# Turning heads and maxima ahead of the projection inside a unit's side work, in an attention and feed-forward block on one core

## The chip, the core and the metric

The kernel runs on one core of a Trainium2 chip. The metric is the device time of one execution in microseconds (us), lower is better. Runs of the kernel before gave 5343.15, 5345.61 and 5349.25 us; their median is 5345.61 us.

The core has five engines with instruction streams of their own. The short names are those of the profile: PE does the matrix products and PEld is its weight load, DVE works on vectors, ACT applies functions, POOL is the general engine and SP only issues transfers here. A matrix product lands in one of the eight banks of the accumulator memory, each 128 partitions by 512 float32, and DVE or ACT reads it from there.

## The reference

The block is pre-normalised attention and then a feed-forward part. The attention has two softmaxes over half heads whose difference is applied to the values:

```python
qkv = x @ w_qkv                                  # x: 8 x 1024 x 512, layer-normed; 16 heads of 32
q1, q2 = split(q); k1, k2 = split(k)             # 16 wide each
a1 = softmax(q1 k1^T * scale); a2 = softmax(q2 k2^T * scale)
lam = exp(lq1 . lk1) - exp(lq2 . lk2) + 0.8
out = (a1 - lam * a2) @ v
out_n = out / sqrt(mean(out^2) + 1e-6) * norm_w * 0.2
x = x + out_cat(out_n) @ wo
```

The feed-forward part rounds its weights to three values, adds a low-rank term, squares a relu and multiplies by a second rounded matrix. The change does not touch it.

## The kernel before

Attention is cut into 256 units: a unit is one batch row, one head and one half (512) of its queries. A unit goes over its 1024 keys in 8 chunks of 128, and the main loop (L561) takes two chunks a step, so a unit has four steps, kc = 0, 2, 4, 6. The order of all instructions on PE, ACT, DVE and POOL is the order in which the loop writes them; nothing is reordered by a scheduler.

Every step has the same main work. `exp_scores` (L253) makes two score tiles for each chunk, one for each softmax: a product that spreads the row maxima (`nms`) over the tile and a product of keys and queries on top of it, both in L267; ACT takes the exponentials (L273). `max_scores` (L197) runs two units ahead: products of the same kind in L207 whose row maxima DVE takes in L218. POOL adds the exponentials up (L283, L285). `values` (L296, product in L290 into `acc`) multiplies the exponentials of the step before by the values.

The first step of a unit, kc = 0, also carries side work, collected in the list `posts`. A side job issues its PE instructions when it is called, and returns a closure with its ACT, DVE and transfer instructions, which all run in the same order at the end of the step:

- `project` (L151, 4 products of 512 columns, which the profile counts as 8 matmuls in L157), then ACT scales (L164), DVE makes the remainder (L165) and SP writes it out. It belongs to the next batch row. `value_tile` (L142, L145) is the same size on PE, with one ACT copy (L149) behind it. Both are marked `long`.
- `max_turn` (L230): one transpose (L232) of the maxima of the next unit, two DVE instructions (L236, L237), one transfer out and two back into `nms`.
- `heads_out` (L318): four transposes (L324) of the output and sums of the unit three before, then two reciprocals, two products and an addition on DVE (L334, L337, L347).
- `sums` (L310): products with ones (L290 into `one`), then an ACT copy (L316).
- `turn_tile` (L134): four transposes (L137) and an ACT copy. It is not `long` and comes last.

`prepare` (L399) lists 35 side steps for a batch row: 3 without PE work, then 8 pairs of a turned tile and a value tile, then 16 projections. One is taken at each kc = 0, and one more at kc = 4 of the 17th, 21st, 25th and 29th unit of a row (L589). The first of these four is a turned tile, the other three are projections, and the side work of kc = 4 has neither maxima nor heads. So a row has 8 value tiles and 13 projections at kc = 0; seven rows are prepared this way, which makes 56 and 91 such steps. Seven turned tiles a row, 49 in all, also lie at kc = 0, and in 27 further steps of kc = 0 with maxima, heads and sums there is no side step of `prepare`. In the last batch row half of the units (`light`, L275) carry two heads or none.

All score tiles and all side jobs draw their banks from one pool of four (`one_bank`, L104). The two chunks of a step take four tiles, so all four banks; the next tile asked for takes the bank of the first score tile, the next that of the second, and so on. A PE instruction that starts a tile therefore waits until the tile that had the bank before has been read. The products of `max_scores` have a pool of three banks of their own, the accumulator `acc` has one.

Of the kernel before, what the change touches and what calls it, by code (L numbers as in the profile page):

```python
# [24 lines left out]
def block_phases(  # L25
# [22 lines left out]
    NU = B * H * 2  # L48
# [55 lines left out]
    def one_bank():  # L104
        return ps_1.tile([P, 512], F32, tag="one", name="one")
# [71 lines left out]
    def load_keys(g):  # L177
        b, h = divmod(g, H)
        tk_of[g] = p_tk.tile([P, S], F32R, tag="tk", name="tk")
        src = qk_of[b][1, h * HD : (h + 1) * HD]  # L180
        for i in range(2):
            nc.sync.dma_start(
                tk_of[g][i::2].bitcast(F32), src[:, i : i + 1, :].to_broadcast([HD, 2, S])
            )

    def load_queries(u):
        b, h = divmod(u // 2, H)
        cols = slice((u % 2) * HS, (u % 2) * HS + HS)
        tq_of[u] = p_tq.tile([P, HS], F32R, tag="tq", name="tq")
        src = qk_of[b][0, h * HD : (h + 1) * HD, :, cols].rearrange("r i t -> (r i) t")  # L190
        for i in range(2):
            nc.sync.dma_start(tq_of[u][i::2].bitcast(F32), src)
# [4 lines left out]
    def max_scores(u, i, apart=False):  # L197

        c, kh = divmod(i, 2)
        if i == 0:  # L200
            nm_of[u] = p_s.tile([P, 2, 2, 4], F32, tag="nm", name="nm", bufs=2)
        mx = [ps_mx.tile([P, 512], F32, tag="mx", name="mx") for _ in range(2)]
        tq, tk = tq_of[u], tk_of[u // 2]

        def product(sm):
            rows = slice(64 * sm, 64 * sm + 64)
            nc.tensor.matmul(  # L207
                mx[sm], tq[rows, c * P : (c + 1) * P],
                tk[rows, kh * 512 : kh * 512 + 512], start=True, stop=True,
            )  # L210

        product(0)
        if not apart:
            product(1)

        def post():
            for sm in range(2):
                nc.vector.tensor_reduce(  # L218
                    nm_of[u][:, kh, sm, c : c + 1], mx[sm], AX.X, ALU.max, negate=True
                )  # L220
            if i == 7:
                nm = nm_of.pop(u)
                nm2_of[u] = p_s.tile([P, 8], F32, tag="nm2", name="nm2", bufs=2)
                nc.vector.tensor_reduce(
                    nm2_of[u], nm.rearrange("p k s c -> p (s c) k"), AX.X, ALU.min
                )

        return (lambda: product(1), post) if apart else post

    def max_turn(u):  # L230
        tr = one_bank()
        nc.tensor.transpose(tr[0:8, 0:P], nm2_of.pop(u), ident)  # L232

        def post():
            mt = p_s.tile([8, 2, P], F32R, tag="mt", name="mt", bufs=2)
            nc.vector.tensor_copy(mt[:, 0, :], tr[0:8, 0:P])  # L236
            nc.vector.tensor_sub(mt[:, 1, :], tr[0:8, 0:P], mt[:, 0, :].bitcast(F32))  # L237
            md = dpool.tile([2, 4, 2, P], F32, tag="md", name="md", bufs=4)
            nc.sync.dma_start(md.rearrange("s c a t -> (s c) a t"), mt.bitcast(F32))
            for sm in range(2):  # L240
                nc.sync.dma_start(
                    nms[u % 3][64 * sm : 64 * sm + 2].bitcast(F32)
                    .rearrange("a (c t) -> a c t", c=4),
                    md[sm].rearrange("c a t -> a c t"),
                )

        return post
# [31 lines left out]
    def add_up(u, kc):  # L279
        e = e_of[u, kc // 2]  # L280
        if kc == 2:
            es_of[u] = p_es.tile([P, 2, 2, HS], F32, tag="es", name="es")
            nc.gpsimd.tensor_add(es_of[u], e_of[u, 0], e)  # L283
        elif kc == 4 or kc == 6 and not light(u):
            nc.gpsimd.tensor_add(es_of[u], es_of[u], e)  # L285
# [19 lines left out]
    def evict(u):  # L305
        avs_of[u] = p_s.tile([P, 2, HS // 2], F32, tag="avs", name="avs", bufs=4)

        nc.scalar.activation(avs_of[u][:, 0, :], acc_of.pop(u), AF.Copy, scale=one_nlam)
# [47 lines left out]
    def rms_squares(n):  # L356
        sq_of[n] = p_y.tile([P, 4, P], F32, tag="sq", name="sq")
        nc.scalar.activation(sq_of[n], og_of[n], AF.Square)

    def rms_sums(n):  # L360
        ss_of[n] = p_s.tile([P, 16], F32, tag="ss", name="ss")
        nc.vector.tensor_reduce(
            ss_of[n], sq_of.pop(n).rearrange("p c (g d) -> p (c g) d", d=HD), AX.X, ALU.add
        )
# [10 lines left out]
    def output_rows(n, bank=one_bank):  # L375
        b, hp = divmod(n, NHP)
        xr = p_y.tile([P, E], F32, tag="xr", name="xr")
        rows = x[b].rearrange("(d r) e -> r d e", d=HD)
        for r in range(4):
            nc.sync.dma_start(xr[32 * r : 32 * r + 32, :], rows[4 * hp + r])  # L380
        py = bank()
        for c in range(KC):
            nc.tensor.matmul(  # L383
                py, og_of[n][:, c, :], wo_sb[:, c, :],
                start=(c == 0), stop=(c == KC - 1),
            )

        def post():
            y = p_y.tile([P, E], F32, tag="y", name="y")
            nc.vector.scalar_tensor_tensor(y, py, nw[:, hp : hp + 1], xr, ALU.mult, ALU.add)  # L390
            nc.sync.dma_start(x1_dram[n // 4][n % 4], y)

        return post
# [46 lines left out]
    with tc.tile_pool(name="a_stage", bufs=1) as stage, tc.manual_schedule(engines=engines):  # L440
# [26 lines left out]
        for i, step in enumerate(steps):  # L467
# [4 lines left out]
            posts = [step()]  # L472
# [7 lines left out]
            if i >= heads:  # L480
                um, im = divmod(i - heads, NS)
# [78 lines left out]
    with tc.tile_pool(name="a_e", bufs=5) as p_e, tc.tile_pool(name="a_es", bufs=2) as p_es:  # L560
        for s in range(0, NS * NU + 2, 2):  # L561
            u, kc = divmod(s, NS)
            um, im = divmod(s + AHEAD, NS)
            if done is not None:
                evict(done)
                done = None
            if u > NU - 2 * H and kc == 0:
                prep.fetch()
            if um < NU:
                if im == 0 and um + 1 < NU:  # L570
                    if um % 2 == 1:
                        load_keys(um // 2 + 1)
                    load_queries(um + 1)
                between, first = max_scores(um, im, apart=True)
            else:
                between = first = None
            if u < NU:
                if u % (2 * H) == 0 and kc == 0:
                    assert not fill
                    fill = prepare(u // (2 * H) + 1) if u + 2 * H < NU else prepare_tokens()  # L580
                exp_scores(u, kc, between=between)
                if first:
                    first()
                exp_scores(u, kc + 1)
                add_up(u, kc)
            reduce = max_scores(um, im + 1) if um < NU else None
            posts = []

            if fill and (kc == 0 or kc == 4 and u % (2 * H) >= H and u % 4 == 0):  # L589
                prepare_step, long = fill.pop(0)  # L590
            else:
                prepare_step = None
            if prepare_step and long:
                posts.append(prepare_step())
            if kc == 0 and um <= NU:
                posts.append(max_turn(um - 1))
            for v in outs.pop((u, kc), []):
                posts.append(heads_out(v))
                if v % 4 == 3:
                    n = v // 4  # L600
                    later[u, 6] = lambda n=n: rms_squares(n)
                    later[u + 1, 0] = lambda n=n: rms_sums(n)
                    later[u + 1, 2] = lambda n=n: rms_apply(n)
                    later[u + 2, 4] = lambda n=n: output_rows(n)
            if (u, kc) in later:
                posts.append(later.pop((u, kc))())
            for v in adds.pop((u, kc), []):
                posts.append(sums(v))
            if prepare_step and not long:
                posts.append(prepare_step())  # L610
            if reduce:
                reduce()
            if 2 <= s < NS * NU + 2:
                uv, kv = divmod(s - 2, NS)
                values(uv, kv)
                values(uv, kv + 1)
                if kv == NS - 2:
                    done = uv
            for post in posts:
                if post:  # L620
                    post()
        evict(done)
        prep.fetch_rest()
        whole(lambda: sums(NU - 1))
# [441 lines left out]
```

## Time and profile before

| What | Value |
|---|---|
| median of three runs | 5345.61 us |
| profiled execution, its own time | 5346.45 us |
| span in the profile | 5344.5 us |
| granted PE clock over the span | 0.999 |
| PE busy | 5277.1 us, 99% |
| DVE busy | 3786.5 us, 71% |
| ACT busy | 2834.1 us, 53% |
| POOL busy | 4128.1 us, 77% |
| of the span, attention steps of the main loop | about 145 to 4260 us |

The span is the time from the first to the last instruction of the program; the profiled execution took 1.95 us more than that. A line of a timeline gives the start in us from the start of the span, the length, the engine (SPq for a transfer issued by SP), the source line, the operation, what it writes and reads, its size and how many equal instructions are merged in the line; in brackets stands the idle time of the engine before it and what ended that time. A line of the waits gives who waited for whom, the total in us, how many times, and the longest.

### The profile page before, as it was taken

How to read it: one execution, taken by the hardware profiler on the slowest of the kernel's cores; microseconds unless marked ns; L12 is line 12 of the kernel's file. 1: busy time of each engine (PE TensorE's matmuls, PEld its weight loads, DVE VectorE, ACT ScalarE, POOL GpSimd, SP SyncE). 2: the span in 40 equal slices, each digit the busy share in tenths (PEclk: the TensorE clock that was granted, in tenths of full speed). 3: DMA queues.
4: the chain of work that ended last, by engine and by line, in shares of the span. 5: the costliest groups of instructions: out<-in, count | busy, mean ns of one | idle time of the engine just before them, and what ended most of it. 6: DMA issues, size and time to landing. Idle time of an engine off the chain costs nothing.

```text
span 5344.5 us, 105614 instructions
## 1 busy us (share of the span) xinstructions
PE 5277.1 (99%) x41522; PEld 3244.8 (61%) x41522; DVE 3786.5 (71%) x7599; ACT 2834.1 (53%) x5502; POOL 4128.1 (77%) x1511
## 2 busy tenths in 40 slices
PE   8999999999999999999999999999999999999999
PEld 4555555555555555555555555555555588788887
DVE  6877787777778777877777777777888545555554
ACT  4665566566656665666566656655666522222221
POOL 0998899889988998899899989998888733333333
PEclk9999999999999999999999999999999999999999
DMA  8112211221121112111211121112211101111111
GB/s 275 49 52 77 69 51 54 75 71 50 55 79 63 52 55 77 64 55 59 77 59 53 63 74 61 52 65 77 97 48 47 60 18 32 32 32 32 32 32 32
DMA packets 185247, 328.49 MB, mean 61 GB/s; under 512 B 33312, under 2 KB 55840, under 8 KB 184112
## 3 DMA queue, kind: packets, MB, share of 16 engines
q1 hardware_dynamic: 183824, 319.12, 18.7%
q8 instruction: 329, 5.39, 0.4%
q0 software_dynamic: 544, 2.10, 0.1%
q14 instruction: 166, 1.36, 0.1%
q10 hardware_dynamic: 384, 0.52, 0.0%
HBM read 209.16 MB, written 112.46 MB: 60 GB/s over the span
## 4 chain that ended last, share of the span: by engine, by line
PE 80%; POOL 12%; DVE 2%; issue 2%; ACT 1%; DMA 1%; SPq 0%; POOLq 0%; DVEq 0%; ACTq 0%
PE acc L290 15%; PE one L267 13%; PE mx L207 12%; PE one L157 8%; PE y L722 7%; POOL es L285 7%; PE pf L708 7%; PE one L290 4%; PE one L145 4%; PE one L383 3%; POOL es L283 3%; PE one L324 2%; DVE nm L218 1%; PE pf L709 1%; ACT e L273 1%
## 5 line engine op out<-in xcount | busy, mean ns | idle before, releaser
L218 DVE TENSOR_REDUCE nm<-mx 128x1 f32<-128x512 f32 x4096 | 2548.4, 682 | 257.6 <-PE mx L207 252.1
L273 ACT ACTIVATE e<-one 128x512 f32<-128x512 f32 x4096 | 2116.8, 602 | 802.8 <-PE one L267 750.5
L285 POOL TENSOR_TENSOR es<-es,e 128x2048 f32<-128x2048 f32 x495 | 2262.6, 4571 | 62.0 <-ACT e L273 30.0
L207 PE MATMUL mx<-tk,tq 64*128 64x512 f32 x4096 | 1451.2, 444 | 6.7 <-DVE nm L218 5.5
L283 POOL TENSOR_TENSOR es<-e 128x2048 f32<-128x2048 f32 x256 | 1170.0, 4570 | 277.1 <-ACT e L273 277.1
L267 PE MATMUL one<-nms,one 64*128 64x512 f32 x4096 | 1177.4, 420 | 4.6 <-ACT e L273 2.7
L290 PE MATMUL acc<-e,v 128*32 128x256 f32 x16384 | 1092.6, 384 | 0.0
L207 PEld LDWEIGHTS mx<-tk,tq 64*128 64x128 f32 x4096 | 751.0, 184 | 546.9 <-DVE nm L218 311.5
L267 PE MATMUL one<-tq,tk 64*128 64x512 f32 x4096 | 1065.0, 393 | 0.0
L712 POOL TENSOR_TENSOR r<-r 128x512 f32<-128x512 f32 x256 | 269.0, 1052 | 644.4 <-ACT r L711 636.7
L290 PEld LDWEIGHTS acc<-e,v 128*32 128x32 f32 x16384 | 450.1, 109 | 433.7 <-issue 177.3
L267 PEld LDWEIGHTS one<-tq,tk 64*128 64x128 f32 x4096 | 580.4, 185 | 83.2
L711 ACT ACTIVATE r<-pf,s_fc 128x512 f32<-128x512 f32 x256 | 176.5, 689 | 793.1 <-PE pf L709 555.8
L267 PEld LDWEIGHTS one<-nms,one 64*128 64x128 f32 x4096 | 515.8, 184 | 79.9 <-DVE og L347 14.7
L722 PE MATMUL y<-wpr,r 128*128 128x512 f32 x2048 | 523.7, 397 | 3.3 <-DVE r L716 1.5
L715 DVE CAST r<-r 128x512 fp32r<-128x512 f32 x256 | 179.0, 699 | 421.9 <-POOL r L712 421.8
L157 PE MATMUL one<-hT,wqk 128*128 128x512 f32 x1024 | 472.8, 605 | 0.0
L722 PEld LDWEIGHTS y<-wpr,r 128*128 128x128 f32 x2048 | 374.8, 188 | 98.6 <-DVE o L732 20.1
L708 PE MATMUL pf<-hTh,wfc 128*128 128x512 f32 x1024 | 399.3, 390 | 0.0
L708 PE MATMUL pf<-hTl,wfc 128*128 128x512 f32 x1024 | 398.9, 390 | 0.0
L165 DVE SCALAR_TENSOR_TENSOR pc<-one,pc 128x512 fp32r<-128x512 f32 x128 | 88.5, 691 | 344.4 <-ACT pc L164 344.4
L157 PEld LDWEIGHTS one<-hT,wqk 128*128 128x128 f32 x1024 | 184.1, 189 | 213.9 <-issue 186.4
(133 smaller groups left out, 4291.6 us busy)
## 6 DMA issues: line engine op xcount, KB each, us to landing
qk<-pc SPq DMA_DIRECT2D x128, 512.0 KB
tk<-qk SPq DMA_DIRECT2D x256, 256.0 KB
tq<-qk SPq DMA_DIRECT2D x512, 128.0 KB
xs<-in_L_attn_x SPq DMA_DIRECT2D x64, 256.0 KB
xr<-in_L_attn_x SPq DMA_DIRECT2D x256, 64.0 KB
x_dram<-y SPq DMA_DIRECT2D x64, 256.0 KB
out<-o SPq DMA_DIRECT2D x248, 64.0 KB
nms<-md SPq DMA_DIRECT2D x512, 4.0 KB
```

The lines of the kernel that those rows point to most:

```text
L145: nc.tensor.matmul(pv, hT_of[b][:, kc, c * P : (c + 1) * P], wv[:, kc, :], start=(kc == 0), stop=(kc == KC - 1),)
L157: nc.tensor.matmul(ps, wqk[:, kc, c0 : c0 + P], hT_of[b][:, kc, tok], start=(kc == 0), stop=(kc == KC - 1),)
L207: nc.tensor.matmul(mx[sm], tq[rows, c * P : (c + 1) * P], tk[rows, kh * 512 : kh * 512 + 512], start=True, stop=True,)
L218: nc.vector.tensor_reduce(nm_of[u][:, kh, sm, c : c + 1], mx[sm], AX.X, ALU.max, negate=True)
L267: nc.tensor.matmul(st[sm], w[rows, cols], m[rows, :], start=(w is one2), stop=(w is not one2))
L273: nc.scalar.activation(e[:, kc % 2, sm, :], st[sm], AF.Exp)
L283: nc.gpsimd.tensor_add(es_of[u], e_of[u, 0], e)
L285: nc.gpsimd.tensor_add(es_of[u], es_of[u], e)
L290: nc.tensor.matmul(out[32 * g : 32 * g + 32, :], w, e[:, g // 2, (g % 2) * (HS // 2) : (g % 2 + 1) * (HS // 2)], start=start, stop=stop,)
L708: nc.tensor.matmul(pf, w[:, kc, :], hT, start=(kc == 0 and i == 0), stop=False)
L712: nc.gpsimd.tensor_mul(r, r, r)
L722: nc.tensor.matmul(ys[i], r2[:, i * P : (i + 1) * P], prep.wpr[j // (NJ // 2)][:, j % (NJ // 2), :], start=(j == 0 and k == 0), stop=(j == ...
```

## The change

Within the side work of a step, `heads_out` is now called first, `max_turn` second, and the long step of `prepare` (a projection or a value tile) third, just ahead of `later` and `sums`. Before, the long step came first, then `max_turn`, then `heads_out`. The order of the closures moves in the same way, so also that of the DVE, ACT and SP instructions behind them. No instruction is added or removed.

```diff
             else:
                 prepare_step = None
-            if prepare_step and long:
-                posts.append(prepare_step())
-            if kc == 0 and um <= NU:
-                posts.append(max_turn(um - 1))
             for v in outs.pop((u, kc), []):
                 posts.append(heads_out(v))
                 if v % 4 == 3:
...
                     later[u + 2, 4] = lambda n=n: output_rows(n)
+            if kc == 0 and um <= NU:
+                posts.append(max_turn(um - 1))
+            if prepare_step and long:
+                posts.append(prepare_step())
             if (u, kc) in later:
                 posts.append(later.pop((u, kc))())
             for v in adds.pop((u, kc), []):
```

## The prediction

> **What bounds the kernel now.** I read the page first, then the waits of PE and DVE, then timelines of single steps.
>
> ```profile
> PE 5277.1 (99%) x41522; PEld 3244.8 (61%) x41522; DVE 3786.5 (71%) x7599; ACT 2834.1 (53%) x5502; POOL 4128.1 (77%) x1511
> ...
> PEclk9999999999999999999999999999999999999999
> ...
> DVE mt L236 <- PE one L232: 154.0, 57, 4.1
> DVE pc L165 <- ACT pc L164: 344.4, 121, 3.9
> PE one L145 <- ACT e L273: 10.7, 12, 1.5
> ```
>
> PE is never idle for long and its clock is full. The long waits are DVE's: it stands behind the projection (344 us, and 154 us before the maxima), with 71% work, so its waits matter only where PE then waits for DVE. A busy PE can still hide held-up instructions, because ends of matmuls are modelled. So I read starts. This is one first step of a unit with a projection, on PE, up to the step after the next:
>
> ```profile
> 1014.93 0.50 PE L207 MATMUL mx<-tk,tq 64*128 64x512 f32 x1
> ...
> 1016.64 3.70 PE L157 MATMUL one<-hT,wqk 128*128 128x512 f32 x8
> 1020.18 0.27 PE L232 MATMUL one<-ident,nm 128*8 128x128 f32 x1
> 1020.29 0.60 PE L324 MATMUL one<-ident,avs 128*128 128x128 f32 x4
> 1020.82 1.07 PE L290 MATMUL one<-es,ones 128*32 128x256 f32 x16
> 1021.70 1.05 PE L290 MATMUL acc<-e,v 128*32 128x256 f32 x16
> 1022.68 0.49 PE L207 MATMUL mx<-tk,tq 64*128 64x512 f32 x1
> ...
> 1025.49 0.50 PE L207 MATMUL mx<-tk,tq 64*128 64x512 f32 x1
> ```
>
> The step takes 7.75 us and every piece follows the last at once: 1.71 main products, 3.54 projection, 0.11 maxima, 0.53 heads, 0.88 sums, 0.98 values. The step behind it takes 2.81 us here, 2.74 in most units (1006.78 to 1009.52), against 2.70 for a plain step (1009.52 to 1012.22). The excess is DVE coming late from the side work. So PE sets the time, and a change of order can matter only through what PE must wait for.
>
> ACT in the same step, its four exponentials and then the third alone, and a step without a projection, where PE visibly waits:
>
> ```profile
> 1015.76 2.06 ACT L273 ACTIVATE e<-one 128x512 f32<-128x512 f32 x4
> 1016.74 0.60 ACT L273 ACTIVATE e<-one 128x512 f32<-128x512 f32 x1
> ...
> 665.04 1.08 ACT L273 ACTIVATE e<-one 128x512 f32<-128x512 f32 x2
> 665.41 0.27 PE L232 MATMUL one<-ident,nm 128*8 128x128 f32 x1
> 665.68 0.42 PEld L324 LDWEIGHTS one<-ident,avs 128*128 128x128 f32 x4 [0.19 <-ACT e L273]
> 665.68 0.66 PE L324 MATMUL one<-ident,avs 128*128 128x128 f32 x4
> 666.27 1.07 PE L290 MATMUL one<-es,ones 128*32 128x256 f32 x16
> ```
>
> Side tiles take the four score banks in turn, so the first needs the first exponential read, the second the second, and so on. In the lower step the maxima are first and the heads second. The second exponential starts at 665.04 and takes 0.60, so it ends at 665.64 (0.01 less if it is 0.59 long); the load of the heads starts at 665.68, 0.05 later, and not 0.11 after the maxima as in the upper step. That is the wait to watch. In the upper step the projection, first in line and 3.54 us long, covers exponentials two to four.
>
> **The change part by part.** Nothing is added or removed on any engine; all is order.
>
> *The 147 steps with a long job (91 projections, 56 value tiles).* Measured from the step's first L207, in us. The heads now start where the projection did, at 1.71: the first exponential has ended at 1015.76 + 0.60 - 1014.93 = 1.43. Their four transposes start 0.11 apart ((0.60 - 0.27) / 3), and the first, whose load nothing covers, costs 0.06 more (0.66 against 0.60 in the two rows). So the maxima follow after 4 x 0.11 + 0.06 = 0.50, at 2.21 (the second exponential is over at about 1.91), and the long job could start at 2.32. But it is third, and the third exponential ends at 1016.74 + 0.60 - 1014.93 = 2.41. With 0.05 for the signal it starts at 2.46: 0.14 of standing.
>
> How long it is then, up to the sums, comes from a step where a projection is followed by an output product of the same size:
>
> ```profile
> 1043.10 3.70 PE L157 MATMUL one<-hT,wqk 128*128 128x512 f32 x8
> 1046.64 3.60 PE L383 MATMUL one<-wo_sb,og 128*128 128x512 f32 x8
> 1050.16 1.07 PE L290 MATMUL acc<-e,v 128*32 128x256 f32 x16
> ```
>
> The first takes 3.54, its first load uncovered (3.70 against 3.60: 0.10). The second, load covered, takes 3.52 to a product of 32-column tiles, 3.44 of it its eight matmuls and 0.08 the passage to that form. A held long job pays both: 3.52 + 0.10 = 3.62. The sums start at 2.46 + 3.62 = 6.08, against 1.71 + 3.54 + 0.11 + 0.53 = 5.89 before. That is +0.19 to +0.20; sums and values follow as before (the fourth exponential is over at 2.89). I take 0.20: 147 x 0.20 = +29.4 us. Bounds: without any hold 2.32 + 3.52 = 5.84, -0.05 a step; with the signal twice as late, +0.25.
>
> [...]
>
> *Late ACT.* In 12 places PE waits for the first exponential before the value tile, up to 1.5 us, because POOL has freed the exponentials' buffer late (ACT's waits for POOL: 26.4 us, 21 times). There the third exponential is 0.97 behind the first while heads and maxima fill 0.61, so the hold is 0.2 longer than in the usual step: +2.5 us.
>
> *DVE behind the step.* Heads (1.2 us) and maxima (0.5) on DVE now run under the projection, and only L165 (0.69) is left behind it. It would end at about 7.6 in a step of 7.95, and the first maximum of the next step starts 0.53 later still. So the excess of the following step goes: by the starts of all 91 such steps it is 0.04 on average, 91 x 0.04 = -3.6 us. This long cover is the change's gain, and it is small because DVE's wait cost PE little.
>
> *The 49 steps with a turned tile and 27 with neither.* Heads and maxima swap, the sums stay third. They start 2.56 after the step's start in the row above; by the new order heads and maxima end at 2.32, the passage to 32 columns takes 0.08, and the third exponential with its signal gives 2.46 to 2.51. About 0.05 is saved, but where the following step is held by DVE (2.74 to 3.2 us: all 27, and 14 of the 49) it comes back, since the DVE work between is the same: 35 x 0.05 = -1.8 us. The 12 steps of the last row with two heads are held by DVE in the same way: 0, between -2 and +2.
>
> *Queues.* On SP the maxima's three transfers now go ahead of the projection's. The write-back is issued when L165 is done, and its readers belong to the next batch row; the maxima are needed a whole unit later, some 8 us: 0. If POOL's adds (three of 4.57 us in a unit of 16) gain slack from longer steps, it is at most a fifth of a us in each of seven rows: 0 to -1.5. ACT's copies of projection and sums come 0.2 later and end about 0.3 before the next step: 0; without that cover the second score pair of the next step would wait for them.
>
> Sum: 29.4 + 2.5 - 3.6 - 1.8 = +26.5. On the profiled execution 5346.45 + 26.5 = 5373. It lies 0.8 us above the median of 5345.61, so 5372 on the scale of the runs.
>
> [...]
>
> **The rivals.** (1) *The load is covered in spite of the hold.* The held time then is the 0.14 less the 0.05 that the order saves, 0.09 to 0.10 a step: 14.7 + 2.5 - 3.6 - 1.8 = +12, 5358. For it: loads and matmuls overlap in most rows. Against it: the held heads above show the uncovered 0.06. (2) *No hold at all, not slower.* If the exponentials or the bank's signal come 0.15 earlier than in the rows, the order saves 0.05 in each of 147 steps: -7.4 - 3.6 - 1.8 = -13, 5333. It decides from the point where the third exponential ends 2.27 or less into the step. Against it: the first exponential waits for its scores on PE, which do not move, and the four follow 0.48 apart in every step I read. (3) *DVE or the output side was already what limits the step,* and PE's standing is taken back by the following steps: 5346, unchanged. Against it: 2.70 us plain steps in which PE has no gap, and L165 with 1.2 us of slack before its bank is needed. (4) *The heads' bank or the late copies hold the next step too.* The copy of the sums ends at 7.6, its bank is needed at about 8.8; if that slack were gone, 0.1 in each of 147 steps more, 5387.
>
> **How the numbers follow.** Forecast (held, +0.20 a step) 0.78, its own range 5363 to 5382 (0.13 to 0.25 a step). Rival 1 0.10, rival 2 0.06, rival 3 0.03, rival 4 0.03. The range 5357 to 5384 takes in the forecast and rival 1. About 0.2%, 10.7 us, is what a measurement can tell from no change: rival 1 lies on that edge and I split it. Slower 0.78 + 0.03 + 0.05 = 0.86, same 0.03 + 0.05 = 0.08, faster 0.06.
>
> **What would show it.** In the profile after: the long job starts about 0.75 after the heads, its load held by ACT e L273; such steps take 7.95 us and the steps behind projections 2.71; DVE no longer waits for L232; PE's clock stays full. A long job starting 0.61 after the heads would prove rival 2, a 7.85 us step rival 1. Steps with turned tiles should be within 0.1 of 5.15.

## The result, and the profile after

The changed kernel takes 5382.58 us (median of 5 runs, 5377.98 to 5383.23), beside 5346.15 us for the kernel before in the same session: a ratio of 1.0065 [1.0054, 1.0077]. It is slower by 36 us where 26 were forecast. The profiled execution took 5383.23 us, its span is 5381.4 us against 5344.5, and the granted clock over the span is 0.997 against 0.999.

The page alone shows little of this. PE is as full as before:

```profile
PE 5304.8 (99%) x41522; PEld 3239.2 (60%) x41522; DVE 3790.6 (70%) x7599; ACT 2832.9 (53%) x5502; POOL 4126.1 (77%) x1511
...
PEclk9999999999999999999999999999999999999999
```

So again the starts have to be read. This is the timeline of PE after the change, for the first step of a unit with a projection, up to the step after the next:

```profile
1021.35 0.50 PE L207 MATMUL mx<-tk,tq 64*128 64x512 f32 x1
...
1023.06 0.66 PE L324 MATMUL one<-ident,avs 128*128 128x128 f32 x4
1023.55 0.27 PE L232 MATMUL one<-ident,nm 128*8 128x128 f32 x1
1023.82 3.70 PE L157 MATMUL one<-hT,wqk 128*128 128x512 f32 x8
1027.45 1.07 PE L290 MATMUL one<-es,ones 128*32 128x256 f32 x16
1028.34 1.05 PE L290 MATMUL acc<-e,v 128*32 128x256 f32 x16
1029.32 0.50 PE L207 MATMUL mx<-tk,tq 64*128 64x512 f32 x1
...
1032.03 0.50 PE L207 MATMUL mx<-tk,tq 64*128 64x512 f32 x1
```

The step takes 1029.32 - 1021.35 = 7.97 us (7.75 before) and the one behind it 2.71. The heads start 1.71 into the step, where the projection started before; the maxima follow 0.49 later; the projection starts at 2.47, 0.27 after the maxima, where it could have come 0.11 after them; and it takes 3.63 up to the sums. The timelines of PE's weight loads and of ACT in the same step name the cause:

```profile
1023.82 0.30 PEld L157 LDWEIGHTS one<-hT,wqk 128*128 128x128 f32 x2 [0.29 <-ACT e L273]
```

```profile
1022.19 2.06 ACT L273 ACTIVATE e<-one 128x512 f32<-128x512 f32 x4
...
1023.16 0.61 ACT L273 ACTIVATE e<-one 128x512 f32<-128x512 f32 x1
```

The second row of ACT is the third exponential. It ends at 1023.16 + 0.61 = 1023.77, and 0.05 later the first load of the projection starts, and its product with it. The projection is third in line for a bank and waits for the third reader.

The views of waits, after, say the same in sum, and also what DVE gained:

```profile
PEld one L324 <- ACT e L273: 72.0, 240, 1.8
...
PE one L324 <- ACT e L273: 12.1, 13, 1.5
...
PE one L145 <- ACT e L273: 2.1, 10, 0.2
...
DVE pc L165 <- ACT pc L164: 255.4, 121, 3.9
```

The first row is the loads of the heads, most of them held under products that still run: PE itself is seen to stand for only the 12.1 us of the second row. DVE's wait for the projection has gone from 344.4 to 255.4 us, and its wait for L232 from 154.0 us to 0.3. PE, which sets the time, got nothing from it but the shorter step behind. The two rows of PE are the places where ACT is late: the long wait is now at the heads (L324), and a second one of 0.2 stands in front of the value tile (L145).

Adding up the starts of all steps in the two traces gives the place of the 36.9 us by which the spans differ:

| Steps | before, us | after, us | difference |
|---|---|---|---|
| 91 with a projection | 705.1 (7.75 each) | 724.3 (7.96) | +19.1 |
| 91 behind them | 250.6 (2.75) | 246.5 (2.71) | -4.1 |
| 56 with a value tile | 445.4 | 460.6 | +15.2 |
| 49 with a turned tile | | | -0.9 |
| two steps late in attention | 7.56 and 6.78 | 9.21 and 8.31 | +3.2 |
| from the start of the last step to the end of the program | 1088.3 | 1091.8 | +3.5 |
| all others | | | +0.9 |

The value tiles' 15.2 are 56 x 0.206 = 11.5 of the held bank, 3.4 from two single steps that became much longer, and about 0.2 on balance from places with a late ACT. Here are both kinds of late place in the timeline of PE after. In the first, ACT is late and the step takes 9.71 us (9.29 before):

```profile
711.04 0.66 PE L324 MATMUL one<-ident,avs 128*128 128x128 f32 x4 [1.47 <-ACT e L273]
711.53 0.27 PE L232 MATMUL one<-ident,nm 128*8 128x128 f32 x1
712.02 3.70 PE L145 MATMUL one<-wv,hT 128*128 128x512 f32 x8 [0.21 <-ACT e L273]
715.65 1.07 PE L290 MATMUL one<-es,ones 128*32 128x256 f32 x16
```

In the second, one batch row later, the same waits stand in the same order, and the step takes 11.41:

```profile
1237.10 0.66 PE L324 MATMUL one<-ident,avs 128*128 128x128 f32 x4 [1.47 <-ACT e L273]
1237.59 0.27 PE L232 MATMUL one<-ident,nm 128*8 128x128 f32 x1
1238.08 5.40 PE L145 MATMUL one<-wv,hT 128*128 128x512 f32 x8 [0.21 <-ACT e L273]
1243.40 1.07 PE L290 MATMUL one<-es,ones 128*32 128x256 f32 x16
```

The same eight matmuls take 5.40 instead of 3.70. The busy time in stretches around it (start and end, length, busy us and instructions of PE, PEld, DVE, ACT and POOL, granted clock, DMA share, GB/s) shows why:

```profile
1233.00:1237.00 4.00, 2.63 (x28) 1.50 (x22) 3.82 (x7) 1.59 (x5) 3.83 (x3) 1.00 0.57 197
1237.00:1241.00 4.00, 3.69 (x10) 1.85 (x11) 1.60 (x7) 1.51 (x4) 3.90 (x3) 0.75 0.03 6
1241.00:1245.00 4.00, 4.00 (x37) 1.62 (x35) 0.00 (x0) 0.96 (x2) 3.83 (x3) 0.83 0.01 2
```

The clock is below 1.00 in the last two stretches. In the traces of both kernels the records behind these means know two values only, 1.00 and 0.50. A record of 0.50 lasts 3.413 us here (once before, seven times after), or 6.827 (once before) or 10.240 (once after), but for the last record of a trace, which reaches past the end of the program. In the kernel before, the same place kept its clock at 1.00 through the late step, although PE stood for 1.47 us there too (1.47 of 4.00 in the first row):

```profile
1226.00:1230.00 4.00, 2.53 (x22) 1.54 (x15) 3.17 (x6) 1.60 (x4) 3.73 (x4) 1.00 0.56 197
1230.00:1234.00 4.00, 4.00 (x21) 1.97 (x23) 0.66 (x4) 1.46 (x3) 4.00 (x2) 1.00 0.00 0
```

Over the program, these records hold 10.24 us of half clock before and 34.13 us after. The page's row, in slices of 135 us, does not show them.

### The profile page after: what moved, and what is told of

The parts are those of the page before. It is cut to its first block, busy times and chain, and to the rows that moved or that the text cites. A ratio compares the mean times of both kernels' runs of the same rounds, so it can differ in the third digit from the quotient of the medians.

```text
span 5381.4 us, 105859 instructions
## 1 busy us (share of the span) xinstructions
PE 5304.8 (99%) x41522; PEld 3239.2 (60%) x41522; DVE 3790.6 (70%) x7599; ACT 2832.9 (53%) x5502; POOL 4126.1 (77%) x1511
## 4 chain that ended last, share of the span: by engine, by line
PE 84%; POOL 11%; DVE 2%; ACT 1%; issue 1%; DMA 0%; SPq 0%; POOLq 0%; DVEq 0%; ACTq 0%
PE acc L290 15%; PE one L267 13%; PE mx L207 13%; PE y L722 9%; PE pf L708 8%; PE one L157 8%; POOL es L285 7%; PE one L290 4%; PE one L145 4%; PE one L383 3%; POOL es L283 3%; PE one L324 2%; PE pf L709 1%; DVE nm L218 1%; ACT e L273 1%
## 5 line engine op out<-in xcount | busy, mean ns | idle before, releaser
L273 ACT ACTIVATE e<-one 128x512 f32<-128x512 f32 x4096 | 2116.4, 603 | 799.7 <-PE one L267 730.8
L285 POOL TENSOR_TENSOR es<-es,e 128x2048 f32<-128x2048 f32 x495 | 2260.8, 4567 | 67.7 <-ACT e L273 35.9
L267 PEld LDWEIGHTS one<-nms,one 64*128 64x128 f32 x4096 | 502.5, 184 | 87.8 <-ACT e L273 16.1
L290 PE MATMUL one<-es,ones 128*32 128x256 f32 x4096 | 274.9, 385 | 14.8 <-POOL es L285 5.3
```

The source lines that it names most:

```text
L267: nc.tensor.matmul(st[sm], w[rows, cols], m[rows, :], start=(w is one2), stop=(w is not one2))
L273: nc.scalar.activation(e[:, kc % 2, sm, :], st[sm], AF.Exp)
L290: nc.tensor.matmul(out[32 * g : 32 * g + 32, :], w, e[:, g // 2, (g % 2) * (HS // 2) : (g % 2 + 1) * (HS // 2)], start=start, stop=stop,)
```

## The experiments

The theory, called H: the place of the long job in the line for the four score banks decides which exponential it waits for, and this is worth what the prediction's numbers say, whatever else is moved. The rival, D: the price lies in the order of DVE's and ACT's work behind the jobs, or in an output side that is late, so that the place of the long job alone is not what counts. The long job is a projection or a value tile.

Each kernel below is shown by its edit to the changed kernel; its ratio is to the kernel before on the same chip.

### The long job second

```diff
                     later[u + 2, 4] = lambda n=n: output_rows(n)
-            if kc == 0 and um <= NU:
-                posts.append(max_turn(um - 1))
             if prepare_step and long:
                 posts.append(prepare_step())
+            if kc == 0 and um <= NU:
+                posts.append(max_turn(um - 1))
```

> Heads first, long job second, maxima third. Theory H (the loss is the wait for the third exponential's bank): the long job now draws the bank of the second exponential, over 1.91 us into the step, and the heads end at 2.21, so nothing is held. The 147 steps take 7.70 us (-0.05 against before), the step behind a projection 2.71, in all 5333 us (5328 to 5340). Rival D (what costs is that the long job starts later behind the main products, so that its copies and the sums come late, whichever bank it draws): the long job still starts 0.5 us later than before, 7.9 us a step, 5368 to 5382.

Measured: 5342.47 us (11 runs), ratio 0.9989 [0.998, 0.9998]. The timeline of PE in a step with a projection, and of its loads:

```profile
1012.72 0.50 PE L207 MATMUL mx<-tk,tq 64*128 64x512 f32 x1
...
1014.43 0.66 PE L324 MATMUL one<-ident,avs 128*128 128x128 f32 x4
1014.93 3.60 PE L157 MATMUL one<-hT,wqk 128*128 128x512 f32 x8
1018.36 0.27 PE L232 MATMUL one<-ident,nm 128*8 128x128 f32 x1
...
1020.43 0.50 PE L207 MATMUL mx<-tk,tq 64*128 64x512 f32 x1
```

```profile
1014.82 0.30 PEld L157 LDWEIGHTS one<-hT,wqk 128*128 128x128 f32 x2
```

The load has no wait in brackets and starts 0.11 ahead of its matmul, which now shows 3.60 and not 3.70. The step takes 7.71, the mean over all of them 7.70 for both kinds, and the step behind a projection 2.71. One short job more or less ahead of the long one is 7.96 against 7.70: H holds and D falls. The total is 10 us above the expected 5333 and 2 above the expected range, although the steps with a long job are as expected. Some 3 us of it are the session: the kernel before took 5348.49 beside it and not 5345.61. Another 3 are two steps late in attention, at half clock here too (9.17 and 8.32). This order beats both kernels, the one before by 0.1%.

### The two short jobs swapped, behind the long one

```diff
+            if prepare_step and long:
+                posts.append(prepare_step())
             for v in outs.pop((u, kc), []):
                 posts.append(heads_out(v))
...
             if kc == 0 and um <= NU:
                 posts.append(max_turn(um - 1))
-            if prepare_step and long:
-                posts.append(prepare_step())
```

> Long job first as before, then heads, then maxima: only these two are swapped, in all steps. Theory H: nothing is held, 7.75 us in the 147 steps; 5344 to 5348. Rival S (the swap of heads and maxima itself costs, in the steps without a long job and at the end of attention, where the traces differ by 1.5 us in single steps): 5350 to 5356.

Measured: 5350.93 us (11 runs), ratio 1.0005 [0.9996, 1.0014]. Steps with a long job take 7.75 as before, those behind a projection 2.76 on average (2.75 before). The swap of heads and maxima is worth nothing to these steps. The total lies above H's expectation and inside that of S, and the two late steps (9.17 and 8.46) are the single steps that S named; but its interval includes no change, so the total doesn't decide. The steps with a long job speak for H. Whether the swap slows the two late steps is taken up again with the run of maxima, long job and heads below.

### The new order for projections only, and for value tiles only

In the first of this pair the value tiles keep their old place, in the second the projections do. In `prepare` the value tile is marked 2 instead of True, and the loop asks for the mark (first kernel shown; the second has 1 and 2 exchanged in the loop):

```diff
+            if prepare_step and long == 2:
+                posts.append(prepare_step())
             for v in outs.pop((u, kc), []):
                 posts.append(heads_out(v))
...
-            if prepare_step and long:
+            if prepare_step and long == 1:
                 posts.append(prepare_step())
```

> The new order in the 91 steps with a projection, the long job first in the 56 with a value tile. Theory H: 91 x 0.21 - 4 = +15, so 5361 us, 7.96 us in projection steps and 7.75 in value tile steps. Theory G beside it (about 10 us of the loss are stretches of 3.4 us at half PE clock, which long waits of PE in the value tile steps behind late exponentials bring about): no such stretch in these steps, and a mean clock of 0.999; if instead the stretches fall by chance anywhere, the clock stays at 0.997 and the time is about 5368.

Measured: 5368.68 us (5 runs), ratio 1.0036 [1.0024, 1.0049]. Steps with a projection take 7.96 (724.2 us in all, as in the changed kernel), those behind 2.71, those with a value tile 7.75; the six late value tiles 9.28 to 9.30, none of them slowed. By the steps alone that is +19.1 - 4.1 = +15.0, as H expected. G was half right: the late value tiles keep their clock, but two late steps of attention (9.04 and 9.33) do not. The mean clock (0.997) and the total, some 5 us above the steps, are those of the other branch of that expectation.

> The new order in the 56 steps with a value tile, the projection first in the other 91. Theory H (wait for the third exponential): 56 x 0.21 + 2.5 = +14, so 5362 us beside 5348 for the kernel before. Theory G (stretches of 3.4 us at half PE clock fall in the value tile steps that wait for late exponentials, since heads and maxima now leave a second gap there): some of the seven value tile steps of 9.3 us take 11.4, and the time is 5364 to 5368; if no such step takes over 10 us, such stretches are chance.

Measured: 5366.27 us (5 runs), ratio 1.0038 [1.0025, 1.0052]. Projection steps are at 7.75, value-tile steps at 7.955, and of the six late ones five take 11.37 to 11.43 and one 9.74. Five times some 1.67 us is 8.4; with 11.5 for the 56 steps that is +20, beside 20.9 measured: G holds here. One late step of attention is slowed too (8.40). The timeline of PE and the busy time in stretches at one of the five:

```profile
1233.55 0.66 PE L324 MATMUL one<-ident,avs 128*128 128x128 f32 x4 [1.48 <-ACT e L273]
...
1234.53 5.35 PE L145 MATMUL one<-wv,hT 128*128 128x512 f32 x8 [0.21 <-ACT e L273]
```

```profile
1233.50:1234.40 0.90, 0.76 (x5) 0.50 (x5) 0.16 (x2) 0.90 (x3) 0.80 (x3) 1.00 0.01 2
1234.60:1237.80 3.20, 3.20 (x4) 1.44 (x5) 1.34 (x5) 0.37 (x1) 3.20 (x1) 0.50 0.04 8
1238.00:1239.00 1.00, 1.00 (x4) 0.52 (x3) 0.00 (x0) 0.00 (x0) 0.83 (x3) 1.00 0.03 8
```

Full clock, then half for one stretch that begins as the value tile does, then full. In the slow stretch PE is busy throughout (3.20 of 3.20): it is the same job at half speed.

### One bank later still

The transpose of the maxima is made twice in the 147 steps, the second time into a bank of its own whose content nobody uses. It costs PE one short transpose and moves the long job to the bank of the fourth exponential.

```diff
-    def max_turn(u):
+    def max_turn(u, again=False):
         tr = one_bank()
-        nc.tensor.transpose(tr[0:8, 0:P], nm2_of.pop(u), ident)
+        nm2 = nm2_of.pop(u)
+        nc.tensor.transpose(tr[0:8, 0:P], nm2, ident)
+        if again:
+            nc.tensor.transpose(one_bank()[0:8, 0:P], nm2, ident)
...
-                posts.append(max_turn(um - 1))
+                posts.append(max_turn(um - 1, prepare_step and long))
```

> The new order with one small transpose of the maxima repeated ahead of the long job in the 147 steps (0.11 us on PE, its result unused), so that the long job draws the fourth exponential's bank. Theory H: the long job starts 0.05 behind the end of the fourth exponential, at 2.94 us instead of 2.46, the steps take 8.44, in all 5382 + 71 = 5453 us. Rival D: only the 0.11 us of work comes on top, 5382 + 16 = 5398 us.

Measured: 5449.67 us (4 runs), ratio 1.0188 [1.0173, 1.0204], within 4 us of H's number and far from D's. The timeline of PE, then of ACT (source lines behind L233 are 3 higher in this kernel):

```profile
1039.24 0.49 PE L207 MATMUL mx<-tk,tq 64*128 64x512 f32 x1
...
1041.43 0.27 PE L233 MATMUL one<-ident,nm 128*8 128x128 f32 x1
1041.69 0.27 PE L235 MATMUL one<-ident,nm 128*8 128x128 f32 x1
1042.18 3.70 PE L157 MATMUL one<-hT,wqk 128*128 128x512 f32 x8 [0.21 <-ACT e L276]
```

```profile
1040.06 2.06 ACT L276 ACTIVATE e<-one 128x512 f32<-128x512 f32 x4
```

The fourth exponential ends at 1040.06 + 2.06 = 1042.12, and the projection starts 0.06 later. One place later in line costs one exponential: 8.44 us a step against 7.96, and 0.48 is the spacing of the exponentials. A short transpose of 0.11 us that computes nothing costs 70.5 us in the 147 steps, because it takes a place in line. Two of the six late value tiles lie at half clock (11.75 and 11.91 us, the others 10.20 to 10.21).

### Maxima, long job, heads

```diff
+            if kc == 0 and um <= NU:
+                posts.append(max_turn(um - 1))
+            if prepare_step and long:
+                posts.append(prepare_step())
             for v in outs.pop((u, kc), []):
                 posts.append(heads_out(v))
...
-            if kc == 0 and um <= NU:
-                posts.append(max_turn(um - 1))
-            if prepare_step and long:
-                posts.append(prepare_step())
```

> Maxima first, long job second, heads third. Theory H: the long job needs the bank of the second exponential, which ends 1.91 us into the step, and the maxima cover only 0.11 of it: it starts at 1.96 instead of 1.82 and its first load is uncovered again, +0.14 a step, 147 x 0.14 = +20, 5368 us beside 5348. Rival D (heads ahead of the long job are what costs): heads stay behind, so within 5 us of the kernel before.

Measured: 5369.25 us (4 runs), ratio 1.0044 [1.0031, 1.0058]; steps with a long job take 7.90, as H worked out, and D's 5 us are far exceeded. The long job is second here as in the first experiment, but the job ahead of it is 0.11 us long and not 0.50, which does not cover the wait for the second exponential. In the timelines of PE and its loads:

```profile
1023.93 0.27 PE L232 MATMUL one<-ident,nm 128*8 128x128 f32 x1
1024.19 3.70 PE L157 MATMUL one<-hT,wqk 128*128 128x512 f32 x8
```

```profile
1024.19 0.30 PEld L157 LDWEIGHTS one<-hT,wqk 128*128 128x128 f32 x2 [0.18 <-ACT e L273]
```

So it isn't the place alone: what counts is whether the short jobs ahead are long enough for the exponential of that place.

### Both kernels again, for the clock

The changed kernel and the kernel before were profiled once more, without an edit.

> The changed kernel once more, beside the others on one chip. Theory H with the half-clock stretches: +30 to +38 over the kernel before, 7.96 us in the 147 steps; the stretches at half clock lie elsewhere than in the first profile if they are chance, in the same steps if waits of PE bring them about.

> The kernel before once more, for a second profile. If stretches at half clock at the end of attention (two single steps 1.5 us longer in every reordered kernel so far) are chance, they show here too; if the swap of heads and maxima brings them, they don't.

Measured: the changed kernel 5378.93 us (5 runs), ratio 1.0061 [1.0048, 1.0073], with the steps of its first trace. Two of its six late value tiles are again at half clock (11.39 and 11.43, the others 9.72 to 9.74), but they are not the two of the first profile. Of the two late steps of attention one is slow (8.47) and one is not (7.52). The kernel before took 5343.65 us in one run; its late value tiles take 9.28 to 9.31, and no late step of attention is slow (7.48 and 6.77).

Counting the late value tiles of all ten traces: where PE stands there once, for some 1.47 us, none of 30 is at half clock (the kernel before twice, and the runs with the long job second, with the short jobs swapped, and with projections only). Where one or two short waits in front of the long job follow the first, 13 of 30 are (the changed kernel twice, value tiles only, one bank later, and maxima, long job and heads). These are not so many independent trials: in the kernel before and with the short jobs swapped, the late steps are 522.1 to 522.7 us apart, about 153 stretches of 3.413 us, so that much the same phase is met six times over. With the long job second (520.8 to 520.9 us, 152.6 stretches) and with projections only (524.3 to 524.4, 153.6) the phases are spread, and none of the twelve is slowed.

What tells the 13 from the others can be read from the traces. The half-clock stretches of a trace start a whole number of 3.413 us apart (in the changed kernel those at 37.47, 1238.96 and 3344.99 us are 1201.49 and 2106.02 us apart, 352 and 617 times 3.4133), so its whole span can be cut into such stretches. Here are two of them at a slowed value tile of the changed kernel, then two at one that kept its clock:

```profile
1235.55:1238.96 3.41, 1.73 (x8) 0.99 (x8) 2.32 (x8) 2.06 (x4) 3.14 (x5) 1.00 0.30 101
1238.96:1242.37 3.41, 3.41 (x5) 1.35 (x4) 0.60 (x3) 0.00 (x0) 3.33 (x2) 0.50 0.05 10
...
1761.16:1764.57 3.41, 2.07 (x20) 1.23 (x12) 3.27 (x7) 1.01 (x4) 3.24 (x3) 1.00 0.75 222
1764.57:1767.99 3.42, 3.07 (x11) 1.61 (x12) 1.60 (x7) 1.55 (x4) 3.32 (x3) 1.00 0.04 15
```

In the first pair both waits fall into one stretch, PE stands for 3.41 - 1.73 = 1.68 us of it, and the next stretch is at half clock. In the second pair the waits are split, 1.3 and 0.3. So it is for all 60: ahead of each of the 13 slow stretches PE stands for 1.63 to 1.80 us within one stretch; at the 47 others it does so for at most 1.53, and in one case 1.66. A wait of 1.47 alone doesn't reach that much, though in 12 of the 30 places it lies whole in one stretch. So in these places the second wait brings the half clock, where it falls into the same stretch as the first.

The steps late in attention differ in phase alone. In all ten traces PE stands there for the same times, 2.57 to 2.66 us for POOL's sums (L285) in the first of the two steps, 0.5 and 1.8 us in the second. Here is the first, in the kernel before and then in the changed one:

```profile
3815.70:3819.11 3.41, 2.20 (x16) 1.18 (x12) 3.38 (x8) 2.91 (x6) 3.33 (x2) 1.00 0.01 4
3819.11:3822.53 3.42, 1.99 (x39) 1.22 (x43) 0.03 (x1) 0.00 (x0) 3.15 (x5) 1.00 0.00 0
...
3846.74:3850.15 3.41, 0.80 (x5) 0.28 (x3) 2.04 (x4) 1.51 (x4) 3.38 (x1) 1.00 0.03 7
3850.15:3853.57 3.42, 3.40 (x32) 1.59 (x36) 0.00 (x0) 0.00 (x0) 3.18 (x4) 0.50 0.00 0
```

Before, the wait is split over two stretches (1.2 and 1.4) and costs no clock; after, it lies in one (2.6), and the next is at half. The run with maxima, long job and heads has the old order in these steps and still takes 9.27 and 8.10 us where the kernel before has 7.56 and 6.78, so the swap of heads and maxima is not what slows them, and S falls in this part. A sharp limit on the standing alone doesn't come out of these steps: the run with value tiles only has 2.0 us in one stretch and keeps its clock, the run with projections only is slowed behind 1.3.

## Why the prediction was right in its direction and short by 10 us

- **PE sets the time, and only its waits count: right.** DVE lost 89 us of waiting for the projection and nearly all of its waiting for L232; PE's part of that was 4.1 us.
- **The 147 steps, +0.20 each: right.** 7.96 in place of the predicted 7.95; the sum of the projection steps gives 0.21, that of the ordinary value-tile steps 0.206. The hold is at the named place, for the named exponential, with the 0.05 of the signal and the 0.10 of the uncovered load: heads to long job 0.76 us (0.75 predicted), long job to sums 3.63 (3.62 predicted). The runs with the long job second (7.70), fourth (8.44) and behind the maxima (7.90) follow from the same numbers.
- **The step behind a projection, -3.6: right**, -4.1 measured; 2.71 us in place of 2.75.
- **Turned tiles, -1.8: the sign right, half the size**, -0.9.
- **Late ACT, +2.5: mis-sized.** Six of the twelve places lost 0.43 each, the 0.2 on top of the usual 0.20 that was supposed; the other six gave that back, and about +0.2 was left on balance, apart from the clock.
- **Queues and copies, 0: right.** No step that follows a long job became longer, which also refutes rival 4 (5387, the next step held too: it takes 2.71 us behind the projection).
- **"PE's clock stays full": this failed.** The terms of the sum, as measured, give 19.1 + 11.5 + 0.2 - 4.1 - 0.9 = about +26, the predicted number; 6.6 more are stretches at half clock, 3.4 us in two late value tiles and 3.2 in two late steps of attention. The remaining 3.5, from the last step on, come and go: the lag is 2.2 at the passage to feed-forward, 0.4 at 4749 us and 4.2 behind a half-clock stretch at 4884 us. The page's clock, 0.999 and then 0.997 over 5381 us, was enough to hide it. That the total stayed near the forecast is in part luck: 5382.58 lies 0.6 us above the forecast's own range (to 5382) and 1.4 below the end of the whole range (5384), and one more value tile at half clock (1.7 us) would have passed both.
- **Rival 1** (5358, a covered load) falls by the 7.96 us step and the load held by L273. **Rival 2** (5333, no hold) falls in the changed kernel; the run with the long job second has the unheld step it describes. **Rival 3** (unchanged) falls by the total.

What stays open is how much of the last two parts (6.7 us together) belongs to the change. The part from the last step on is 1088.3 and 1085.2 us in the two profiles of the kernel before, 1091.8 and 1088.2 in those of the changed kernel, so it moves by as much without any change. The two late steps lose by the phase in which they meet the clock's stretches, and the kernel before spreads over 5343 to 5354 us in 35 runs. A run that moves the whole program by a few us against the clock's stretches, with no other change, was not tried.

## What to carry to other kernels

With an in-order engine and a small ring of banks, ask of each side job how many jobs are ahead of it in the ring and which reader it therefore waits for, and how long the work ahead of it is. Short work belongs ahead of a long job only as far as it fills the wait for the long job's own bank: here one job of 0.5 us ahead is free and gains 0.05 us a step, two cost 0.21, one of 0.11 us costs 0.15, and three cost 0.69. An engine with 99% busy time can still be standing, as PE was here for 1.47 us at a time, so read starts; and beside such a wait a second short one can cost more than its length, through the clock: here 1.7 us for one of 0.21 behind one of 1.47, in 13 of 30 places, each time with both in one stretch of 3.413 us.

## What was not expected of the hardware

The granted clock fell to 0.50 for 3.413 us in 13 of 30 late value tiles where PE had stood for 1.47 and then 0.21 us, with 0.3 to 0.8 us of matmuls between, and never in the 30 late value tiles with 1.47 us alone. The five slow value tiles of the run with the new order for value tiles only are 525.3 to 525.7 us apart, the length of a batch row, and that is 153.9 to 154.0 stretches of 3.413 us, so that they meet the clock's stretch in nearly the same phase each time; in the changed kernel the late steps are 526 to 528 us apart, their phases differ, and two of the six are at half clock, not the same two in two executions.

Nothing in the traces says how the clock is granted. They show what went ahead of the half clock in all 13: a stretch of 3.413 us in which PE stood for 1.63 to 1.80 us, in two or three pieces. One such stretch with 1.66 us was followed by full clock.
